# Two graph-attention layers: bias and beta added two batches ahead, key sums added by pairs, and VectorE's pieces moved within the step

## The chip, the cores and the metric

The kernel runs on one core of one Trainium2 chip. The core has a matrix engine (TensorE, PE in the profile), a vector engine (VectorE, DVE), a scalar engine (ScalarE, ACT), a general engine (GpSimd, POOL) and SyncE (SP), which here issues DMAs and waits. Each works through its own queue in order. The metric is the device time of one execution in microseconds (us).

## What is computed

`x` has 8 batches of 2048 nodes with 256 features, and one 2048 x 2048 adjacency matrix (`adj`, 0 or 1) serves all of them. Two layers follow each other, all in float32. Cut to what matters:

```python
# layer 0: attention with 4 heads of 64, softmax within each chunk of 256 keys, summed over the 8 chunks
h = maximum(layernorm(x), 0)
q, k, v = h @ Wq.T + bq, h @ Wk.T + bk, h @ Wv.T + bv
scores = clip(q.k / 8, -10, 10);  scores = where(adj == 0, -10, scores)
attn = softmax(scores, within the chunk);  ctx = sum over chunks of attn @ v
out = ctx @ Wo.T + bo + h
x = x + layernorm(out) * gamma + beta
# layer 1: one head, softmax over all keys
h = maximum(layernorm(x), 0) @ W
e = leaky_relu(h.a1 [of the node] + h.a2 [of the key]);  e = where(adj == 0, -1e9, e)
x = x + relu(softmax(e) @ h)
```

## The kernel before, in words

Batches run one after another, each in three stretches. **Attention** (layer 0) has 32 steps `n`: four blocks of 512 queries (`nb`) times eight chunks of 256 keys (`j`). **The passage** finishes the last block and makes layer 1's features while the next batch's queries, keys and values are computed. **Layer 1's products** take 16 pieces, four blocks of 512 queries times four groups of 512 keys.

The order on every engine is written out by hand in the body of the function. A step of attention does, for each of the four heads: the logits (PE, L502) into a two-bank PSUM tile `ps_s`, of which there are two; the clip against the bounds, which carry the mask (DVE, `clip`, L549), into a tile `e` of 2 x 512 per partition (11 in a ring, `ES`); the exponential in place (ACT, L557); and the addition of the two key halves (POOL, `add`, L564) into `g`. One DMA that accumulates, issued by POOL (`fold`, L569), adds one half of the partitions to the other; PE sums over partitions (L539); ACT makes reciprocals (`invert`, L575, L576). PE multiplies by the values (L517), DVE scales (`scale`, L588), and for all chunks but a block's first another accumulating DMA of POOL (`gather`, L592) adds the product `prod` to `ctxT`.

These are staggered: `begin(f)` and `end(f)` are the halves of step f. In them stand clips 3 of step f-1 and 0 of step f (begin), clips 1 and 2 of step f (end), and sums and values of step f-2. Each half calls a list of *pieces*, work of other stretches put beside attention. A piece with place 2f+2 stands in `begin(f)`, one with 2f+3 in `end(f)`; a plain piece stands at the end of its half, behind the half's two clips, and in `end` also behind the scaling. The places of a block's pieces are counted from 16 places after the block's first (`Between.beside`, `at((nb + 1) * PER + n)`).

The pieces of a finished block (class `Between`) are: load of x (-3), `residual`, a second normalization of x (ACT, L375; 3 and 4), `bias` (POOL, L756; 5 and 6), `beta` (POOL, L778; 8 and 10), the output projection (PE, L735; 9 and 10), `take`, which adds the projection to the biased features (DVE, L749; 10), statistics (DVE, L351 and L352; 11 and 12), `gamma` (DVE, L767; 14 and 15), scaling (ACT, L774), `add` to x (POOL, L782; 18 and 20), then layer 1's statistics, normalization and `flip1`, a transpose of 32 x 32 squares (DVE, L138; 30 and 31), and `send1`, which puts them into DRAM. The last block's pieces stand around the end of attention. In batch 0, further pieces prepare batch 1 (`beats`: load, statistics, normalization, flip, send) and turn the rest of the adjacency.

SP issues the loads, among them the bounds of the next block (L176, 1 MB, `fetch`), and carries in each step two empty instructions (`fence`, L471) that wait for PE's accumulator groups, so that SP keeps pace with PE.

In layer 1's products, DVE makes weights two pieces ahead: `weights` (L966: max of two scaled rows; L970: mask) into two tiles `e` of 2 x 512 per piece. PE multiplies (L988), and after each block `finish` divides, applies relu (ACT, L1009) and adds to x (POOL, L1011). Beside them the batch two ahead (`far`) is loaded into a tile `xp`, normalized, flipped and sent to DRAM; x is loaded again when its block is finished. The last four pieces also carry the first step of the next batch's attention (`early`).

Of the kernel before, what the change touches and what calls it, by code (L numbers as in the profile page):

```python
# [26 lines left out]
ES = 11  # L27
# [3 lines left out]
def gnn_two_layers(  # L31
# [96 lines left out]

    class Turning:
# [48 lines left out]

    def store_bounds(nb):
        nc.sync.dma_start(bound_d[nb], bounds[nb])  # L180
# [21 lines left out]
    def load_x(b, nb, tag, bufs):  # L202
        if tag == "g":
            if nb == 0:
                of_setup.append(g_tile())
            t = of_setup[0][:, nb * TB * F:(nb + 1) * TB * F].rearrange("p (t f) -> p t f", t=TB)
        else:
            t = xpool.tile([P, TB, F], F32, tag=tag, name=tag, bufs=bufs)
        nc.sync.dma_start(t, x[b, nb * NB:(nb + 1) * NB, :].rearrange("(p t) f -> p t f", p=P))
        return t  # L210
# [3 lines left out]
    def hn_tile(name="hn"):  # L214
        return work.tile([P, 2, F], F32, tag="hn", name=name, bufs=5)
# [59 lines left out]
    def missing_of(rows, t, half):  # L275

        tag = "e" if in_setup[0] else "hn"
        z = work.tile([P, 2 if in_setup[0] else 1, HALF], BF16, tag=tag, name="z", bufs=ES if tag == "e" else 5)
# [109 lines left out]
    class Projection:  # L388
        def __init__(self, b):
            self.b = b  # L390
            self.q = self.k = self.v = None
            self.adder = nc.vector
            self.x, self.mv, self.rn, self.hns, self.hT, self.pt = ({} for _ in range(6))

        def load(self, nb):
            self.x[nb] = load_x(self.b, nb, *(("g", 1) if in_setup[0] else ("xp", 1)))
# [6 lines left out]
        def power(self, nb):  # L403
            norm_power(self.mv[nb], self.rn[nb])

# [72 lines left out]
    class Attention:  # L478
# [28 lines left out]
        def values(self, n, half, turn, kt):  # L507
# [7 lines left out]
            for h in range(HEADS):  # L515
                at = h * DH + c * Q
                made.append(nc.tensor.matmul(  # L517
                    self.num[n, c][h * Q:(h + 1) * Q, :], self.v[rows, j * KT + kt, at:at + Q],
                    self.e[n, self.ORDER.index((h // 2, h % 2))][rows, kt, :],
                    start=turn == 0 and kt == 0, stop=turn == 1 and kt == KT - 1,  # L520
                ))
# [22 lines left out]
        def clip(self, n, o):  # L544
            if not self.has(n):
                return
            nb, j = self.STEPS[n]
            self.e[n, o] = work.tile([P, KT, NB], F32, tag="e", name="e", bufs=ES)
            nc.vector.scalar_tensor_tensor(  # L549
                self.e[n, o], self.s.pop((n, o)), -CLIP * SC,  # L550
# [3 lines left out]
        def exponentials(self, n, o):  # L554

            if self.has(n):
                nc.scalar.activation(self.e[n, o], self.e[n, o], AF.Exp, scale=1.0 / SC)  # L557

        def add(self, n, o):

            if self.has(n):
                p, i = self.ORDER[o]
                e = self.e[n, o]
                nc.gpsimd.tensor_tensor(self.both(n)[:, 2 * p + i, :], e[:, 0, :], e[:, 1, :], op=ALU.add)  # L564
# [25 lines left out]
        def gather(self, n):  # L590
            if self.has(n) and self.STEPS[n][1] > 0:
# [40 lines left out]
        def begin(self, f, pieces=()):  # L632
# [15 lines left out]
            if f == 1:  # L648
                for o in range(3):
                    self.add(0, o)  # L650
            self.add(f - 1, 3)
            self.fold(f - 1)
            if odd:
                self.slots(f, "o10", "v11", "o11", "o20")
            else:
                self.slots(f, "o10", "s00", "o11", "o20")
                self.add(f, 0)
            self.run(pieces, None)

        def end(self, f, pieces=()):  # L660
            odd = f % 2
            self.run(pieces, "first")
            if odd:
                self.slots(f, "s00", "o21", "v20", "v30", "v21", "v31")
                self.add(f, 0)
# [7 lines left out]
            self.add(f, 1)  # L673
# [8 lines left out]
            self.gather(f - 2)  # L682
            self.add(f, 2)
# [10 lines left out]
    class Between:  # L694
# [6 lines left out]
        def load(self):  # L701
            self.x4 = load_x(self.proj.b, self.nb, "x", NNB)

        def residual(self, t2):
            self.hn0[t2] = normed(self.x4, self.proj.rn[self.nb], t2)
# [39 lines left out]
        def take(self, t2):  # L745
            if t2 == 0:
                self.o4 = work.tile([P, TB, F], F32, tag="o4", name="o4", bufs=1)
                self.mv, self.rn = norm_tiles("rn", 2 * NNB)
            nc.vector.tensor_tensor(  # L749
                self.o4[:, 2 * t2:2 * t2 + 2, :], self.pp[t2].rearrange("p (i f) -> p i f", i=2),  # L750
                self.hn0[t2], op=ALU.add,
            )

        def bias(self, t2):
            hn = self.hn0[t2]
            self.adder.tensor_tensor(hn, hn, bo_r[:, None, :].to_broadcast([P, 2, F]), op=ALU.add)  # L756
# [19 lines left out]
        def beta(self, t2):  # L776
            x2 = self.x4[:, 2 * t2:2 * t2 + 2, :]
            self.adder.tensor_tensor(x2, x2, beta_r[:, None, :].to_broadcast([P, 2, F]), op=ALU.add)  # L778
# [77 lines left out]
        def beside(self):  # L856
# [8 lines left out]
                9: [pe1(lambda: self.output_tiled(0))],  # L865
                10: [
                    pe(lambda: self.output_tiled(1)), lambda: self.take(0), lambda: self.take(1),
                    lambda: self.beta(1),
                ],
                11: [lambda: self.stats([0, 1])],  # L870
                12: [lambda: self.stats([2, 3])],
                13: [self.power],
                14: [lambda: self.gamma([0, 1])],
                15: [lambda: self.gamma([2, 3])],
                16: [lambda: self.scaled(range(TB))],
                18: [lambda: self.add(0)],
                20: [lambda: self.add(1)],
# [5 lines left out]
            if self.nb == NNB - 2:  # L883
                return todo
            at(22, lambda: self.stats1([0, 1]))
            at(24, lambda: self.stats1([2, 3]))
            at(26, self.power1)
            at(27, self.shift1)
            at(28, lambda: self.norm1(0))
# [13 lines left out]
    class Layer1:  # L903
# [39 lines left out]
        def source(self, nb, of_keys):  # L943
            self.src[nb] = work.tile([P, NB], F32, tag="hn", name="src", bufs=5)
# [15 lines left out]
        def weights(self, nb, j4):  # L960
            made = []
            for i in range(2):
                w = work.tile([P, 2, NB], F32, tag="e", name="w", bufs=ES)
                at = 4 * j4 + 2 * i
                for j in (at, at + 1):
                    nc.vector.tensor_scalar(  # L966
                        w[:, j - at, :], self.src[nb], self.cd[:, 0, j:j + 1], self.cd[:, 1, j:j + 1],
                        op0=ALU.mult, op1=ALU.max,
                    )
                nc.vector.scalar_tensor_tensor(  # L970
                    w, bounds1[nb][:, at:at + 2, :], 0.0, w, op0=ALU.is_gt, op1=ALU.mult
                )
                made.append(w)
            return made
# [6 lines left out]
        def products(self, accs, w, j4):  # L981
# [4 lines left out]
            for i, t in pairs:  # L986
                j = 4 * j4 + i
                nc.tensor.matmul(  # L988
                    accs[t][:, 0:F + 1], w[i // 2][:, i % 2, t * P:(t + 1) * P], g[0][:, j, :],
# [153 lines left out]
    for b in range(B):  # L1143
# [25 lines left out]
        if b == 0:  # L1169
# [3 lines left out]
            beats = [(12, 13, 18, 19), (31, 32, 33, 34), (44, 46, 47, 48), (57, 58, 59, 60)]  # L1173
            for nb, ns in enumerate(beats):
                at(ns[0] - 5, lambda nb=nb: ahead.load(nb))
                for t, n in enumerate(ns):
                    at(n, lambda nb=nb, t=t: ahead.stats(nb, [t]))
                n = ns[-1]
                at(n + 1, lambda nb=nb: ahead.power(nb))
                at(n + 2, lambda nb=nb: ahead.shift(nb))  # L1180
                at(n + 3, lambda nb=nb: ahead.norm(nb, 0))
                at(n + 4, lambda nb=nb: ahead.norm(nb, 1))
                at(n + 4, lambda nb=nb: ahead.flip(nb, 0))
                at(n + 5, lambda nb=nb: ahead.flip(nb, 1))
                at(n + 7, lambda nb=nb: ahead.send(nb))
        else:
            at(6, lambda: fetch(bounds, 1))
        at(PER + 4, lambda: fetch(bounds, 2))
        at(2 * PER + 4, lambda: fetch(bounds, 3))
        at(3 * PER + 4, lambda: fetch(bounds1, 0))  # L1190
        at(STEPS2 + 2, lambda: fetch(bounds1, 1))
        at(STEPS2 - 6, last.load)
        at(STEPS2, lambda: last.residual(0))

        late = 0 if ahead else 2
        at(STEPS2 + 1 + late, lambda: last.residual(1))
        at(STEPS2 + 2, lambda: last.bias(0))
        at(STEPS2 + 3 + late, lambda: last.bias(1))
        at(STEPS2 + 4, lambda: last.beta(0))
        at(STEPS2 + 5, lambda: last.beta(1))  # L1200
# [147 lines left out]
        for i, (nb, j4) in enumerate(pieces1):  # L1348
# [21 lines left out]
            if far and i in (3, 6, 9, 12):  # L1370
                far.send(i // 3 - 1)
            if far and i in (0, 3, 6, 9):
                far.load(i // 3)
            if far and i in (1, 4, 7, 10):
# [48 lines left out]
```

## Time and profile before

| what | value |
|---|---|
| median of 3 runs | 3776.11 us (3771.88 to 3776.38) |
| the profiled execution | 3785.24 us, span 3783.5 us |
| granted TensorE clock | 0.984 |
| busy: PE, DVE, POOL, ACT | 3549.0, 2715.3, 2066.2, 1948.6 us |
| attention of batch 2, first to last clip | 295.1 us (1018.9 to 1314.0) |
| passage of batch 2 | 70.5 us (1314.0 to 1384.5) |
| layer 1's products of batch 2, to the next batch's first clip | 93.9 us (1384.5 to 1478.4) |

In the profile's group lines, after the operation and its tiles (out<-in), come the shapes (partitions x elements), the count, the union of the busy times in us, the mean of one in ns, and the idle time of the engine just before the group with what ended most of it. In a timeline come start, length, engine, line, operation, tiles and count; the bracket has the idle time before and who ended it. In a list of waits come the waiting instruction, whom it waited for, the sum in us, how often, and the longest. In a table of stretches the busy times of PE, PEld (weight loads), DVE, ACT and POOL follow the length, and last come the granted clock, the busy share of the DMA engines and GB/s.

### The profile page before, as it was taken

To read this page: it belongs to the slowest core of one execution; us is meant where nothing else is said; L and a number is where in the kernel's file an instruction comes from. 1 tells how busy PE (TensorE), PEld (TensorE's weight loads), DVE (VectorE), ACT (ScalarE), POOL (GpSimd) and SP (SyncE) were. 2 spreads that over 40 slices of the span, in tenths; PEclk is the share of its full clock that TensorE was granted. 3 is DMA by queue.
4 is the path that set the end of the run, shared out by engine and by line. 5 is a ranking of instruction groups with operands and counts; after the bars stand their busy time and mean duration, and the time that the engine had idled before them with its cause. 6 is when DMAs were issued, how large, how long until landed. Compare 5 with 4: busy or idle time off the path is not lost. (4 is left out here: it accounts for less than half of the span.)

```text
span 3783.5 us, 101129 instructions
## 1 busy us (share of the span) xinstructions
PE 3549.0 (94%) x44032; PEld 2085.4 (55%) x44032; DVE 2715.3 (72%) x4083; ACT 1948.6 (52%) x2929; POOL 2066.2 (55%) x1885
## 2 busy tenths in 40 slices
PE   8998999989999999998999999999999999999989
PEld 4334684446844477444764448644485445854458
DVE  6878586785768766786767767677676775757856
ACT  5666425674266632676336753366623665146641
POOL 3777107881088811887038860388504884058831
PEclk9999999999999999999999999999999999999989
DMA  7777526674367742777427764377643766147731
GB/s 225 160 147 152 112 92 127 127 148 99 92 135 140 156 92 76 153 140 155 99 72 146 147 141 89 88 136 146 141 97 89 148 130 143 56 85 146 145 78 51
DMA packets 189580, 463.76 MB, mean 123 GB/s; under 512 B 39760, under 2 KB 101456, under 8 KB 164560
## 3 DMA queue, kind: packets, MB, share of 16 engines
q0 software_dynamic: 53120, 252.74, 37.5%
q1 hardware_dynamic: 127696, 203.51, 18.9%
q8 instruction: 345, 5.65, 0.6%
q10 hardware_dynamic: 8320, 1.05, 0.2%
q14 instruction: 99, 0.81, 0.1%
HBM read 154.14 MB, written 51.43 MB: 54 GB/s over the span
## 5 line engine op out<-in xcount | busy, mean ns | idle before, releaser
L564 POOL TENSOR_TENSOR g<-e 128x512 f32<-128x512 f32 x1024 | 1466.5, 1483 | 473.2 <-ACT e L557 218.1
L502 PE MATMUL ps_s<-q,k 64*32 64x512 f32 x16384 | 1511.2, 602 | 90.6 <-DVE e L549 89.9
L549 DVE SCALAR_TENSOR_TENSOR e<-ps_s,bound 128x1024 f32<-128x1024 f32 x1024 | 1215.0, 1218 | 517.0 <-PE ps_s L502 497.4
L557 ACT ACTIVATE e<-e 128x1024 f32<-128x1024 f32 x1024 | 1064.7, 1053 | 666.4 <-DVE e L549 638.9
L517 PE MATMUL ps_n<-e,v 64*32 64x512 f32 x16384 | 1374.9, 601 | 12.3 <-ACT r L1009 7.6
L502 PEld LDWEIGHTS ps_s<-q,k 64*32 64x32 f32 x16384 | 469.1, 107 | 669.0 <-issue 300.0
L517 PEld LDWEIGHTS ps_n<-e,v 64*32 64x32 f32 x16384 | 472.7, 108 | 433.6 <-issue 246.8
L988 PE MATMUL ps_s<-g,w 128*128 128x257 f32 x2048 | 448.0, 380 | 0.0
L588 DVE TENSOR_TENSOR prod<-ps_n,rz 128x512 f32<-128x512 f32 x448 | 287.6, 684 | 192.7 <-PE ps_n L517 89.4
L988 PEld LDWEIGHTS ps_s<-g,w 128*128 128x128 f32 x2048 | 389.1, 190 | 56.2
L539 PE MATMUL ps_t<-g,ones 64*32 64x512 f32 x2048 | 284.1, 622 | 95.7 <-DMA g<-g 91.3
L363 POOL TENSOR_TENSOR krn<-krn,mv 128x4 f32<-128x4 f32 x28 | 6.6, 237 | 589.4 <-DVE w L966 589.4
L970 DVE SCALAR_TENSOR_TENSOR w<-bound,w 128x1024 f32<-128x1024 int8 x256 | 314.7, 1229 | 8.7
L1011 POOL TENSOR_TENSOR x<-x,r 128x256 f32<-128x256 f32 x124 | 92.0, 786 | 408.1 <-ACT r L1009 407.3
L988 PE MATMUL ps_n<-g,w 128*128 128x257 f32 x1024 | 292.4, 382 | 0.0
L988 PE MATMUL ps_t<-g,w 128*128 128x257 f32 x1024 | 289.7, 379 | 0.0
L966 DVE TENSOR_SCALAR w<-src,cd 128x512 f32<-128x512 f32 x512 | 263.3, 556 | 7.0 <-ACT src L945 6.6
L575 ACT ACTIVATE rz<-ps_t 128x512 f32<-128x512 f32 x256 | 151.0, 590 | 220.0 <-PE ps_s L502 124.8
L569 POOL DMA_DIRECT2D g<-g x256 | 212.8, 831 | 78.9 <-POOL g L564 63.8
L592 POOL DMA_DIRECT2D ctxT<-prod x224 | 206.0, 920 | 76.7 <-DVE prod L588 57.1
L988 PEld LDWEIGHTS ps_n<-g,w 128*128 128x128 f32 x1024 | 192.9, 190 | 44.3 <-issue 17.6
L988 PEld LDWEIGHTS ps_t<-g,w 128*128 128x128 f32 x1024 | 193.8, 189 | 28.2
(133 smaller groups left out, 3004.7 us busy)
## 6 DMA issues: line engine op xcount, KB each, us to landing
g<-g POOLq DMA_DIRECT2D x256, 512.0 KB, 5.6
ctxT<-prod POOLq DMA_DIRECT2D x224, 512.0 KB, 5.2
bound<-bound_d SPq DMA_DIRECT2D x62, 1024.0 KB, 6.9
turned_d<-squares SPq DMA_DIRECT2D x232, 128.0 KB, 2.4
hT<-turned_d SPq DMA_DIRECT2D x58, 512.0 KB, 4.0
rows<-in_adj_dram SPq DMA_DIRECT2D x32, 512.0 KB, 5.6
x<-in_x_dram SPq DMA_DIRECT2D x32, 512.0 KB, 4.5
out_dram<-x SPq DMA_DIRECT2D x31, 512.0 KB, 2.6
```

Of the source, the lines that this page charges most:

```text
L502: nc.tensor.matmul(self.s[n, o][c * Q:(c + 1) * Q, kt, :], self.k[p][rows, at:at + Q], self.q[p][rows, nb * NB:(nb + 1) * NB], start=True, ...
L517: made.append(nc.tensor.matmul(self.num[n, c][h * Q:(h + 1) * Q, :], self.v[rows, j * KT + kt, at:at + Q], self.e[n, self.ORDER.index((h / ...
L539: nc.tensor.matmul(self.total[n][h * Q:(h + 1) * Q, :], ones[rows, :], self.both(n)[rows, h, :], start=True, stop=True,)
L549: nc.vector.scalar_tensor_tensor(self.e[n, o], self.s.pop((n, o)), -CLIP * SC, bounds[nb][:, j * KT:(j + 1) * KT, :], op0=ALU.max, op1=ALU ...
L557: nc.scalar.activation(self.e[n, o], self.e[n, o], AF.Exp, scale=1.0 / SC)
L564: nc.gpsimd.tensor_tensor(self.both(n)[:, 2 * p + i, :], e[:, 0, :], e[:, 1, :], op=ALU.add)
L569: nc.gpsimd.dma_start(self.both(n)[mine], self.both(n)[other], accum_op=ALU.add)
L588: nc.vector.tensor_tensor(dst[:, c, :], self.num.pop((n, c)), self.rz[n], op=ALU.mult)
L592: nc.gpsimd.dma_start(self.ctxT[self.STEPS[n][0]], self.prod.pop(n), accum_op=ALU.add)
L966: nc.vector.tensor_scalar(w[:, j - at, :], self.src[nb], self.cd[:, 0, j:j + 1], self.cd[:, 1, j:j + 1], op0=ALU.mult, op1=ALU.max,)
L970: nc.vector.scalar_tensor_tensor(w, bounds1[nb][:, at:at + 2, :], 0.0, w, op0=ALU.is_gt, op1=ALU.mult)
L988: nc.tensor.matmul(accs[t][:, 0:F + 1], w[i // 2][:, i % 2, t * P:(t + 1) * P], g[0][:, j, :], start=j == 0, stop=j == NT - 1,)
```

## The change

It has four parts, and what follows from them.

- **Bias and beta.** While layer 1's products of batch b run, the normalized features and the x of batch b+2 get `bo` and `beta` added on POOL (`ready`) and are stored in DRAM (`keep_ready`, tensors `hb` and `xb`). A finished block of batches 1 to 7 then loads `hb` into `o4` (`features`, place 7) and `xb` into `x4` (`load`), and `residual`, `bias` and `beta` fall away there. `take` adds the projection to `o4` in place. For batch 1, x is loaded and normalized once more in layer 1 of batch 0. In batch 0 normalization and both additions stay, at other places.
- **Pairs.** A tile `e` holds both heads of a pair (4 x 512; 6 in the ring). In odd steps POOL adds the key halves of each pair in one instruction of 128x1024; in even steps it does so for pair 0 and keeps two single ones for pair 1. The gather of even steps moves from `end(f)` to behind the fold of `begin(f + 1)`.
- **Pieces of VectorE.** Statistics, `gamma` and the flips now stand in `begin` halves (places 12 and 14, 16 and 18, 30 and 32). In batch 0 the statistics for batch 1 are made by ACT (`moments`).
- **Bounds in parts.** The fetches within attention go out in four parts of 256 KB, one in every second half step.

A tile `xp` is no longer kept: x of the batch ahead goes into the rings `e` (layer 1) or `hT` (batch 0's attention). The weights of a piece are one tile of 4 x 512. The diff, cut to its core:

```diff
-ES = 11
+ES = 6
+    def fetch_part(of, nb, part):
+        if part == 0:
+            of[nb] = bound_tile()
+        four = slice(part * NT // 4, (part + 1) * NT // 4)
+        nc.sync.dma_start(of[nb][:, four, :], bound_d[nb][:, four, :])
...
+        def moments(self, nb, part):
...
+                for t in tiles:
+                    nc.scalar.activation(self.scratch[:, t % 2, :], x[:, t, :], AF.Copy, accum_out=mv[:, t, 0:1])
...
+        def ready(self, nb):
+            x = self.x[nb]
+            for t2 in range(2):
+                two = slice(2 * t2, 2 * t2 + 2)
+                hn, x2 = self.hns[nb][t2], x[:, two, :]
+                nc.gpsimd.tensor_tensor(hn, hn, bo_r[:, None, :].to_broadcast([P, 2, F]), op=ALU.add)
+                nc.gpsimd.tensor_tensor(x2, x2, beta_r[:, None, :].to_broadcast([P, 2, F]), op=ALU.add)
+        def keep_ready(self, nb):
+            d = ready_d[self.b % 2]
+            for t2 in range(2):
+                nc.sync.dma_start(d["hb"][nb][:, 2 * t2:2 * t2 + 2, :], self.hns[nb][t2])
+            nc.sync.dma_start(d["xb"][nb], self.x[nb])
...
-        def add(self, n, o):
+        def add(self, n, p, i=None):
             if self.has(n):
-                nc.gpsimd.tensor_tensor(self.both(n)[:, 2 * p + i, :], e[:, 0, :], e[:, 1, :], op=ALU.add)
+                e = self.e[n, p].rearrange("p (i k) q -> p k i q", k=KT)
+                heads = slice(0, 2) if i is None else slice(i, i + 1)
+                nc.gpsimd.tensor_tensor(
+                    self.both(n)[:, 2 * p:2 * p + 2, :][:, heads, :], e[:, 0, heads], e[:, 1, heads], op=ALU.add
+                )
...
         def begin(self, f, pieces=()):
-            self.add(f - 1, 3)
-            self.fold(f - 1)
+            if odd:
+                self.add(f - 1, 1, 0)
+                self.fold(f - 1)
+                self.gather(f - 3)
+            else:
+                self.add(f - 1, 1)
+                self.fold(f - 1)
...
         def end(self, f, pieces=()):
-            self.add(f, 1)
+            self.add(f, 0)
...
-            self.gather(f - 2)
-            self.add(f, 2)
+            if odd or not self.has(f + 1):
+                self.gather(f - 2)
+            else:
+                self.add(f, 1, 1)
...
-                3: [lambda: self.residual(0)],
-                4: [lambda: self.residual(1)],
-                5: [lambda: self.bias(0)],
-                6: [lambda: self.bias(1)],
-                8: [lambda: self.beta(0)],
-                11: [lambda: self.stats([0, 1])],
-                12: [lambda: self.stats([2, 3])],
-                14: [lambda: self.gamma([0, 1])],
-                15: [lambda: self.gamma([2, 3])],
+                7: [self.features],
+                12: [lambda: self.stats([0, 1])],
+                14: [lambda: self.stats([2, 3])],
+                16: [lambda: self.gamma([0, 1])],
+                17: [lambda: self.scaled([0, 1])],
+                18: [lambda: self.gamma([2, 3]), lambda: self.add(0)],
+                19: [lambda: self.scaled([2, 3])],
...
-            at(31, lambda: self.flip1(1))
+            at(32, lambda: self.flip1(1))
...
-        at(PER + 4, lambda: fetch(bounds, 2))
+        for part in range(4):
+            at(PER + 4 + 2 * part, lambda part=part: fetch_part(bounds, 2, part))
...
             if far and i in (3, 6, 9, 12):
                 far.send(i // 3 - 1)
+                far.ready(i // 3 - 1)
+            if far and i in (4, 7, 10, 13):
+                far.keep_ready(i // 3 - 1)
...
+            if b == 0 and i in (3, 6, 9, 12):
+                for t2 in range(2):
+                    ahead.norm(i // 3 - 1, t2)
+                ahead.ready(i // 3 - 1)
```

More of the change, by code (lines that the diff above doesn't have):

```diff
@@ L127, in gnn_two_layers @@
     }
+    ready_d = [
+        {name: [kept.tile([P, TB, F], F32, name=f"{name}_d{i}_{nb}") for nb in range(NNB)] for name in ("hb", "xb")}
+        for i in range(2)
+    ]
     class Turning:
@@ L943, in source @@
         def source(self, nb, of_keys):
-            self.src[nb] = work.tile([P, NB], F32, tag="hn", name="src", bufs=5)
+            self.src[nb] = work.tile([P, NB], F32, tag="hn", name="src", bufs=HS)
             nc.scalar.activation(
@@ L960, in weights @@
         def weights(self, nb, j4):
[L961 to L968, printed above, removed]
-                    )
[L970 to L974, printed above, removed]
+            w = work.tile([P, 4, NB], F32, tag="e", name="w", bufs=ES)
+            for i in range(4):
+                j = 4 * j4 + i
+                nc.vector.tensor_scalar(
+                    w[:, i, :], self.src[nb], self.cd[:, 0, j:j + 1], self.cd[:, 1, j:j + 1],
+                    op0=ALU.mult, op1=ALU.max,
+                )
+                if i % 2:
+                    two = w[:, i - 1:i + 1, :]
+                    nc.vector.scalar_tensor_tensor(
+                        two, bounds1[nb][:, j - 1:j + 1, :], 0.0, two, op0=ALU.is_gt, op1=ALU.mult
+                    )
+            return w
         def accumulators(self, nb):
@@ L1191, in gnn_two_layers @@
+        for part in range(4):
+            at(PER + 4 + 2 * part, lambda part=part: fetch_part(bounds, 2, part))
+            at(2 * PER + 4 + 2 * part, lambda part=part: fetch_part(bounds, 3, part))
+            at(3 * PER + 4 + 2 * part, lambda part=part: fetch_part(bounds1, 0, part))
         at(STEPS2 + 2, lambda: fetch(bounds1, 1))
         at(STEPS2 - 6, last.load)
-        at(STEPS2, lambda: last.residual(0))
-        late = 0 if ahead else 2
-        at(STEPS2 + 1 + late, lambda: last.residual(1))
@@ L1197, in gnn_two_layers @@
[L1197 to L1200, printed above, removed]
+        at(STEPS2 + 5, last.features)
+        for t2 in range(2):
+            at(STEPS2 + 3 + t2, lambda t2=t2: last.beta(t2))
+            at(STEPS2 + 5, lambda t2=t2: last.bias(t2))
         at(STEPS2 + 3, low.fetch1)
```

148 lines of the change are left out of this document (92 added, 56 removed).

## The prediction, made before the changed kernel ran

> **What bounds the kernel now.** I read the page first, then who waited for whom on PE, then one batch in stretches, then single waits in order of time.
>
> ```profile
> PE 3549.0 (94%) x44032; PEld 2085.4 (55%) x44032; DVE 2715.3 (72%) x4083; ACT 1948.6 (52%) x2929; POOL 2066.2 (55%) x1885
> ...
> L564 POOL TENSOR_TENSOR g<-e 128x512 f32<-128x512 f32 x1024 | 1466.5, 1483 | 473.2 <-ACT e L557 218.1
> ...
> L539 PE MATMUL ps_t<-g,ones 64*32 64x512 f32 x2048 | 284.1, 622 | 95.7 <-DMA g<-g 91.3
> ```
>
> TensorE bounds the kernel. What can be won without less TensorE work is its idle time, 234 us, and PE's own waits say who causes it: the fold that adds two halves of the softmax sums (L569, awaited by L539), and VectorE's clips, which must free a PSUM bank before the next logits (L502).
>
> ```profile
> PE ps_t L539 <- DMA g<-g: 91.3, 69, 6.4
> PE ps_s L502 <- DVE e L549: 89.9, 68, 3.4
> ```
>
> By stretches, batch 2: attention (first to last clip), the passage, and layer 1's products.
>
> ```profile
> 1018.90:1314.00 295.10, 273.36 (x4660) 136.75 (x4660) 218.54 (x262) 186.38 (x239) 233.02 (x205) 0.99 0.66 130
> 1314.00:1384.50 70.50, 66.75 (x349) 41.32 (x350) 29.85 (x77) 35.37 (x81) 13.45 (x13) 1.00 0.56 118
> 1384.50:1478.40 93.90, 93.90 (x458) 80.67 (x456) 84.24 (x164) 17.66 (x42) 9.38 (x16) 1.00 0.37 101
> ```
>
> After each length come the busy times of PE, PEld, DVE, ACT, POOL. Attention has 21.7 us of PE idle and a POOL at 79%. In layer 1 PE has none, POOL is nearly free, but DVE is at 90%: the change moves POOL work there.
>
> An idle microsecond costs more than itself. Eight of the small matmuls start every 0.43 us; at that pace attention's need about 255 of the 295.1 us, so 40 are lost where 21.7 are idle. [...] I count a wait taken away at 1.3 to 1.4 times its length (between 1 and 40/21.7 = 1.8).
>
> Where the two waits come from:
>
> ```profile
> 1101.95 0.32 SPq L176 DMA_DIRECT2D bound<-bound_d  x1
> ...
> 1103.73 0.83 POOL L569 DMA_DIRECT2D g<-g  x1 [0.30 <-POOL g L564]
> ...
> 1112.13 0.63 PE L539 MATMUL ps_t<-g,ones 64*32 64x512 f32 x4 [1.59 <-DMA g<-g]
> ```
>
> This fold was issued 1.78 us behind a 1 MB fetch of bounds and landed after 8.27 us; with no fetch in its way one takes 5.11. The batch has three such waits (1.59, 1.51, 1.03 = 4.1 us). Three more (0.88, 0.34, 0.69 = 1.9) follow steps in which additions of bias, beta and x stand on POOL ahead of the key sums: there the fold goes out some 3 us after the last exponential, where 1.69 is usual. The rest, an x load and the stretch's start, stays.
>
> ```profile
> 1159.19 2.85 DVE L767 SCALAR_TENSOR_TENSOR o<-o,mv,gamma_r 128x256 f32<-128x256 f32 x2
> 1161.96 2.34 DVE L549 SCALAR_TENSOR_TENSOR e<-ps_s,bound 128x1024 f32<-128x1024 f32 x2
> ```
>
> ```profile
> 1163.23 0.63 PE L502 MATMUL ps_s<-q,k 64*32 64x512 f32 x4 [2.32 <-DVE e L549]
> ```
>
> Two gamma pieces stand between the second and the last clip of a step, and PE waits 2.32 us. Alone one takes 0.47 us; beside a POOL addition it is held until that ends (0.91 in the mean of all). The batch has three such waits (2.32, 2.71, 2.99) and three of 0.62 behind statistics: 9.9 us.
>
> **The change, part by part.** Sums are against the profiled execution, 3785.24 us (span 3783.5 and 1.7 around it), 9.1 above the median of 3776.11.
>
> *Bounds in four parts* (31 fetches of attention; the batch's three above among them). They are spaced, since SP carries a fence (L471) for every accumulator group and waited 1900 us in all at them. A quarter takes about a quarter of the fetch's 3.2 us from a fold: 4.1 falls to about 1.2 per batch.
>
> *Bias and beta out of attention.* 64 additions at L756 (1575 ns) and 64 at L778 (1543) were on POOL, four per block; batch 0's 16 stay. So 1.9 falls to about 0.2. ACT loses four normalizations per block (587 ns each), which were hidden. In their place each of 28 blocks fetches o4, 0.5 MB more on SP's queue beside a fold. An x load of that size made the fold at 1079.54 land after 7.25 us and cost 1.45; others cost nothing. I take 0.3 each, **8 us** (0 to 40).
>
> Fold together: (2.9 + 1.7) x 1.3 = 6 per batch, seven batches, **-42** (0 to -70).
>
> *Pairs.* 1024 additions become 384 of 128x1024 and 256 of 128x512; the trace has no such pair. A lone 128x512 takes 1.31, a lone 128x256 0.73, so the slope gives 2.5; two queued ones take 2.82. POOL gains 0.3 per pair, but is not the last in a steady step. For odd steps the fold then follows the last exponential by 2.8 rather than 1.7, which the half step until their sums covers: such folds landed 3 to 5 us early with no fetch in the way. Even steps, which have no such room, keep a single last addition, and their gather moves behind the fold. Zero, with 0.3 per step (77 us for 256) as the bad end and the POOL time won back as the good one, inside the fold's -70.
>
> *VectorE's pieces behind the first clips.* Statistics, gamma and flips now follow the two clips that begin a step, and the next bank is wanted later. There L767's pair took 1.94 us at 1153.87 with no wait of PE after it. New is that in even steps the second gamma pair stands beside a pair addition, and can be held 2.5 instead of 1.3: I leave 2 us per batch of 9.9. 7.9 x 1.4 = 11 per batch, **-76**; batch 0, whose statistics for batch 1 go from DVE (32 operations) to ACT, had 20.0 us of this wait in attention and I take half, **-10** (together 0 to -125).
>
> *Larger e tiles, fewer.* Six of 4x512 for eleven of 2x512, and none for xp. A clip needs the tile of three steps ago, released before its logits: zero. In layer 1 three weights and two x tiles share the six; covered by VectorE's lead, below.
>
> *Additions in layer 1.* 28 blocks x 4 additions of 128x512: 24 blocks beside the products of batches 0 to 5 for the batch two ahead, and 4 more, for batch 1, in batch 0's. POOL is free, but VectorE's weights are held meanwhile:
>
> ```profile
> 1469.45 3.11 POOL L1011 TENSOR_TENSOR x<-x,r 128x256 f32<-128x256 f32 x4 [9.76 <-ACT r L1009]
> ```
>
> ```profile
> 1470.99 1.85 DVE L966 TENSOR_SCALAR w<-src,cd 128x512 f32<-128x512 f32 x2
> ...
> 1474.02 1.00 DVE L966 TENSOR_SCALAR w<-src,cd 128x512 f32<-128x512 f32 x2
> ```
>
> Two L966 lost 0.86 us to about 1.54 of POOL time, 56%. One block's additions are 4 x 1.31 = 5.2 us, so DVE loses 2.9 (0 if they fall on statistics and transposes, 5.2 if all is lost). Weights lead the products by 7 to 15 us, which covers it. The first thing late is the passage to the next batch: the clips of its step 0 stand behind weights(15), and PE takes them after the next products.
>
> ```profile
> 1478.48 2.35 DVE L549 SCALAR_TENSOR_TENSOR e<-ps_s,bound 128x1024 f32<-128x1024 f32 x2 [2.20 <-PE ps_s L502]
> ```
>
> They end at 1480.83 and are wanted at 1485.50: with the 2.20 idle before, 6.9 us to spare. Four blocks make 11.6, a stall of 4.7 in batches 1 to 5; batch 0, with eight, 23.2 - 6.9 = 16. **+40** (0 to 5 x 13.9 + 35 = 104).
>
> The rule here is in the Trainium skill, "Advanced Engine Details and Errata", section VectorE Performance Modes: the second VectorE port is shared with GpSimd, and the instructions of one block those of the other. It names no share. Read as all of the time lost it gives the 104; the row's 56% gives the 40, and I go by the row.
>
> Stores of the prepared tiles (28 MB) fall on layer 1, whose DMA engines are 37% busy: zero.
>
> Sum: -42 - 76 - 10 + 8 + 40 = -80: 3705.2 profiled, and 9.1 less by the median: **3696 us**.
>
> **Rivals.**
> 1. *The held weights stay covered* (additions fall on statistics and transposes): -128 + 8 = -120, 3656. For it: 7 to 15 us of lead. Against: DVE is at 90% there. Chance 0.25.
> 2. *The forecast*, 3696, its own range 3672 to 3728. 0.42.
> 3. *Attention gives half*: the even folds, which have almost no room, become the limit as soon as VectorE is not. -64 + 48 = -16 to, with the additions covered, -56: 3720 to 3760, say 3745. For it: even folds often land 0.14 us before their sums start. 0.18.
> 4. *Slower: POOL's hold on VectorE costs its full price.* All of an addition's time is lost to the weights (+104), and a gamma piece behind a 2.5 us pair addition waits so long that PE's clip waits come back (the -86 gone): -42 + 8 + 104 = +70, 3846. With the clip waits back it turns slower from 2.7 us of hold per block (28 holds less the 41.4 to spare reach 34); with them gone only from 5.8. Against: the 56%, and that the DMA issue behind an odd step's single addition leaves the port free. 0.12.
> 5. *The parts go out together*, SP being ahead: 2.9 x 1.3 x 7 = 26 less won, 3722. Against: the fences. 0.03.
>
> **How the numbers follow.** 0.2% (7.6 us) is about what a measurement of this kernel can tell from no change. Rivals 1, 2, 5 and most of 3 are faster: 0.83; a slim part of 3 falls within: 0.04; 4 and what I have not seen: 0.13. The range takes in 1 with some room below, all of 2, 3 and 5, and leaves out 4: 3638 to 3785.
>
> **What would show it.** PE's wait for the fold falls from 91.3 to about 55, that for the clips from 89.9 to about 50, less what the end of layer 1 adds; POOL's key sums show 384 pairs near 2.5 us; the folds behind bounds land in 6 us instead of 8; the weights' L966 and L970 grow in the mean, and a wait of PE for the first clips of each batch appears while layer 1's last products run, longest in batch 0. I am wrong if the sums' wait stays near 91, if that first-clip wait passes 15 us in every batch, or if a steady pair of steps becomes longer than now.

## The result, and the profile after

The changed kernel takes 4029.32 us (median of 4 runs, 4027.72 to 4040.25), the kernel before 3776.24 (4 runs): a ratio of 1.068 (95% interval 1.066 to 1.070), 253 us slower. The forecast was 3696, 80 us faster, and its range ended at 3785. The profiled execution took 4029.38 us, its span 4027.6.

The page of the changed kernel; the columns are those explained with the profile before:

```profile
PE 3626.2 (90%) x44032; PEld 2082.3 (52%) x44032; DVE 2880.3 (72%) x4051; ACT 1920.9 (48%) x2897; POOL 2034.2 (51%) x1501
...
L622 POOL TENSOR_TENSOR g<-e 128x1024 f32<-128x1024 f32 (+1 forms) x640 | 1290.6, 2084 | 474.3 <-ACT e L615 309.5
...
L593 PE MATMUL ps_t<-g,ones 64*32 64x512 f32 x2048 | 300.2, 655 | 293.7 <-DMA g<-g 249.2
...
L652 POOL DMA_DIRECT2D ctxT<-prod x224 | 220.2, 983 | 405.3 <-DMA ctxT<-prod 93.6
...
ctxT<-prod POOLq DMA_DIRECT2D x224, 512.0 KB, 6.3
```

TensorE is idle for 401 us where it was for 234. POOL has less to add, as was meant (its key sums, L622, fell from 1466.5 to 1290.6 us), and nothing is won by it: POOL now stands idle for 405 us in front of the gathers. Before, the gather's two rows read:

```profile
L592 POOL DMA_DIRECT2D ctxT<-prod x224 | 206.0, 920 | 76.7 <-DVE prod L588 57.1
...
ctxT<-prod POOLq DMA_DIRECT2D x224, 512.0 KB, 5.2
```

PE's waits in the changed kernel (waiting instruction, whom it waited for, sum in us, times, longest):

```profile
PE ps_t L593 <- DMA g<-g: 249.2, 99, 7.1
PE ps_t L593 <- POOL g L622: 38.7, 13, 5.0
PE ps_s L556 <- DVE e L605: 32.6, 26, 2.6
PE ps_s L556 <- ACT r L1080: 26.2, 7, 6.6
```

The third row is what the change was to bring: the clips' wait fell from 89.9 to 32.6. The first is what it cost: the sums' wait rose from 91.3 to 249.2. The last row did not exist before; it belongs to layer 1.

**Where the time goes, step by step.** A stretch of batch 2 in the changed kernel, in order of time:

```profile
1222.11 0.81 POOL L629 DMA_DIRECT2D g<-g  x1 [0.30 <-POOL g L622]
1222.66 1.17 POOL L652 DMA_DIRECT2D ctxT<-prod  x1
...
1225.05 2.44 POOL L622 TENSOR_TENSOR g<-e 128x1024 f32<-128x1024 f32 x1 [1.22 <-ACT e L615]
...
1227.37 2.19 ACT L615 ACTIVATE e<-e 128x1024 f32<-128x1024 f32 x2 [1.46 <-DVE e L605]
...
1231.04 0.86 POOL L652 DMA_DIRECT2D ctxT<-prod  x1 [3.55 <-PE ps_s L556]
...
1231.63 2.69 POOL L622 TENSOR_TENSOR g<-e 128x1024 f32<-128x1024 f32 x1
...
1234.62 0.83 POOL L629 DMA_DIRECT2D g<-g  x1 [0.30 <-PE ps_s L556]
...
1239.87 0.94 PE L593 MATMUL ps_t<-g,ones 64*32 64x512 f32 x4 [2.90 <-DMA g<-g]
```

The gather of an even step goes out at 1222.66, right behind a fold, and lands at 1230.49, 7.8 us later. The next gather adds into the same `ctxT` and must not start before. Its product is ready at 1225.74, yet it is issued at 1231.04, 0.55 us after that landing. (The bracket names PE's logits, with which a gather has nothing to do; where the named engine can't be the reason, it was another, here the DMA.) POOL works in order, so the pair's addition and the fold behind it wait too, although the last exponential they need ended at 1228.42 (the first of the two in the row of ACT): the fold lands at 1239.73, and PE, 2.90 us idle, takes the sums at 1239.87. By the trace's DMA records, 88 of the 192 gathers that follow another into the same tile start 0.3 to 0.8 us after its landing, against 6 before. The gathers of steps 2, 4 and 6 of a block land 8.3, 8.0 and 7.8 us after their issue (5.0, 4.9, 6.7 before); the folds land as they did (5.76 us in even and 5.79 in odd steps, from 5.74 and 6.27).

**What an idle microsecond costs.** These stretches of the same step show it (length, then busy times of PE, PEld, DVE, ACT, POOL, granted clock, DMA share, GB/s):

```profile
1236.90:1239.87 2.97, 0.07 (x5) 0.03 (x2) 2.97 (x1) 0.00 (x0) 2.97 (x3) 1.00 0.71 132
1239.87:1243.30 3.43, 3.43 (x40) 1.40 (x48) 3.36 (x4) 1.54 (x3) 2.12 (x3) 0.53 0.54 79
```

PE stands idle for 2.90 of these 2.97 us, and for the next 3.43 it is granted about half its clock (0.53). Over the whole trace, a stretch at half clock began within 5 us of the end of 53 of 56 idle stretches of PE of 3 us or more, of 9 of 29 between 2 and 3 us, and of 2 of 64 between 0.5 and 2 us. The Trainium skill, "TensorE: Matmul & The Clock Gate", section Why this matters for your kernels, advises against gaps of more than about 3 us between matmuls for this reason; the trace agrees. In the kernel before it was 5 of 6, 17 of 32 and 10 of 98, so 3 us is no sharp limit here. So every span in this text is split in three: PE's idle time (span less PE's busy time), the clock's loss (span times the missing share of the clock), and the rest.

| kernel | span | idle | clock | rest |
|---|---|---|---|---|
| before | 3783.5 | 234.5 | 61 (0.984) | 3488 |
| changed | 4027.6 | 401.4 | 153 (0.962) | 3473 |

Of 244 us more, 167 are idle time and 92 the clock. Half clock that falls into idle time is counted in both columns; counted only while PE is busy, the clock's loss is 56 and 134 us, 78 more, and the rest is the same in both kernels (3493 and 3492).

### The profile page after: what moved, and what is told of

It is laid out like the page before. It is cut to its first block, busy times and chain, and to the rows that moved or that the text cites. A ratio compares the mean times of both kernels' runs of the same rounds, so it can differ in the third digit from the quotient of the medians.

```text
span 4027.6 us, 101085 instructions
## 1 busy us (share of the span) xinstructions
PE 3626.2 (90%) x44032; PEld 2082.3 (52%) x44032; DVE 2880.3 (72%) x4051; ACT 1920.9 (48%) x2897; POOL 2034.2 (51%) x1501
## 5 line engine op out<-in xcount | busy, mean ns | idle before, releaser
L556 PE MATMUL ps_s<-q,k 64*32 64x512 f32 x16384 | 1539.1, 606 | 60.5 <-DVE e L605 32.6
L622 POOL TENSOR_TENSOR g<-e 128x1024 f32<-128x1024 f32 (+1 forms) x640 | 1290.6, 2084 | 474.3 <-ACT e L615 309.5
L571 PE MATMUL ps_n<-e,v 64*32 64x512 f32 x16384 | 1390.9, 627 | 8.8 <-ACT r L1080 7.6
L556 PEld LDWEIGHTS ps_s<-q,k 64*32 64x32 f32 x16384 | 463.6, 108 | 637.1 <-issue 340.3
L593 PE MATMUL ps_t<-g,ones 64*32 64x512 f32 x2048 | 300.2, 655 | 293.7 <-DMA g<-g 249.2
L652 POOL DMA_DIRECT2D ctxT<-prod x224 | 220.2, 983 | 405.3 <-DMA ctxT<-prod 93.6
L1042 DVE SCALAR_TENSOR_TENSOR w<-bound,w 128x1024 f32<-128x1024 int8 x256 | 345.8, 1351 | 8.8
L1036 DVE TENSOR_SCALAR w<-src,cd 128x512 f32<-128x512 f32 x512 | 325.3, 677 | 7.0 <-ACT src L1017 6.6
L593 PEld LDWEIGHTS ps_t<-g,ones 64*32 64x32 f32 x2048 | 56.6, 108 | 431.8 <-POOL g L622 277.2
```

What stands on the lines that cost most here:

```text
L556: nc.tensor.matmul(self.s[n, o][c * Q:(c + 1) * Q, kt, :], self.k[p][rows, at:at + Q], self.q[p][rows, nb * NB:(nb + 1) * NB], start=True, ...
L571: made.append(nc.tensor.matmul(self.num[n, c][h * Q:(h + 1) * Q, :], self.v[rows, j * KT + kt, at:at + Q], self.e[n, h // 2][rows, h % 2 * ...
L593: nc.tensor.matmul(self.total[n][h * Q:(h + 1) * Q, :], ones[rows, :], self.both(n)[rows, h, :], start=True, stop=True,)
L622: nc.gpsimd.tensor_tensor(self.both(n)[:, 2 * p:2 * p + 2, :][:, heads, :], e[:, 0, heads], e[:, 1, heads], op=ALU.add)
L652: nc.gpsimd.dma_start(self.ctxT[self.STEPS[n][0]], self.prod.pop(n), accum_op=ALU.add)
L1036: nc.vector.tensor_scalar(w[:, i, :], self.src[nb], self.cd[:, 0, j:j + 1], self.cd[:, 1, j:j + 1], op0=ALU.mult, op1=ALU.max,)
```

## The experiments

**1. The gather back in its place** (the changed kernel otherwise):

```diff
         def begin(self, f, pieces=()):
             if odd:
                 self.add(f - 1, 1, 0)
                 self.fold(f - 1)
-                self.gather(f - 3)
...
         def end(self, f, pieces=()):
-            if odd or not self.has(f + 1):
-                self.gather(f - 2)
-            else:
+            self.gather(f - 2)
+            if not odd and self.has(f + 1):
                 self.add(f, 1, 1)
```

> The changed kernel, but the gather of even steps stands again in end(f), in front of the single key-sum addition. Theory A (the moved gather lands late behind the fold, the next gather into the same ctxT must wait for its landing, and POOL, standing in that wait, sends the odd fold late): the odd gathers' 395 us of idle before them go, PE's wait for the fold falls from 249 us to 60 or less, and the time to 3640 to 3730. Theory B (pairs make the odd folds late): still above 3950. Theory C (the additions in layer 1 hold VectorE): still above 3900.

Measured: 3808.93 us, 1.0075 of before (1.0048 to 1.0102). 220 of the 253 us are gone, the clock is 0.981, and 11 gathers instead of 88 start right behind a landing. So theory A names the main cause, but the time is in no theory's range, and the sums' wait stays at 117.9 us where 60 or less were expected. The kernel is still not faster than before; the rest of the forecast had failed too, by less.

**2. Only the gather moved, in the kernel before** (the same edit in the other direction).

> The kernel before, with one edit: the gather of even steps moves behind the fold of the next begin. Theory A: this edit alone costs what the change cost, 3930 to 4050, with odd gathers starting 0.55 us after the landing of the one before. Theories B and C: within 20 us of the kernel before.

Measured: 4025.9 us, 1.0654 (1.0621 to 1.0687). This one move, with nothing else changed, makes the kernel as slow as the whole change did: 245 us here, 220 in the changed kernel, whose other parts cost 28 in sum (experiment 1). POOL's idle time before gathers is 460.9 us, and PE waits:

```profile
L592 POOL DMA_DIRECT2D ctxT<-prod x224 | 223.8, 999 | 460.9 <-PE ps_n L517 164.2
```

```profile
PE ps_t L539 <- DMA g<-g: 258.7, 118, 8.5
PE ps_s L502 <- DVE e L549: 68.8, 63, 4.2
```

**3. The gather in the same half step, ahead of the addition and the fold.**

```diff
             if odd:
+                self.gather(f - 3)
                 self.add(f - 1, 1, 0)
                 self.fold(f - 1)
-                self.gather(f - 3)
```

> The changed kernel with the gather of even steps in the same half step, but ahead of that half's single addition and fold instead of behind them. Theory A (what costs is that the next gather, which accumulates into the same ctxT, must wait for this one's landing, and this one lands late because it stands behind the fold): issued about 2 us earlier and with no fold ahead of it, it lands near 5 us after issue instead of 8, POOL's idle time before gathers falls from 405 us to below 150, and the time to 3800 to 3880 (3809 is the kernel with the gather fully back; the odd folds still go out 0.9 us later behind it). Rival (any place in the next step costs as much, since the two gathers still stand three quarters of a step or less apart): 3950 or more.

Measured: 3868.5 us, 1.0235 (1.0199 to 1.0271), inside the first theory's 3800 to 3880. POOL's idle time before gathers fell to 124 us, and gathers land after 5.5 us in the median; those of steps 2, 4 and 6, the moved ones, after 6.7, 5.2 and 6.5 in the mean (8.3, 8.0 and 7.8 behind the fold):

```profile
L652 POOL DMA_DIRECT2D ctxT<-prod x224 | 187.2, 836 | 123.8 <-DVE prod L648 43.2
...
ctxT<-prod POOLq DMA_DIRECT2D x224, 512.0 KB, 5.5
```

So it is the landing that the next gather waits for, made late by the fold in front. A quarter of the gathers (47) still start right behind a landing, and the fold now stands behind the gather: the sums' wait is 158.2 us, 117.9 with the gather fully back.

**4. Every head added by itself** (on experiment 1: the pair's one instruction of 128x1024 becomes two of 128x512 at the same place).

```diff
-                heads = slice(0, 2) if i is None else slice(i, i + 1)
-                nc.gpsimd.tensor_tensor(self.both(n)[...][:, heads, :], e[:, 0, heads], e[:, 1, heads], op=ALU.add)
+                for one in (1, 0) if i is None else (i,):
+                    nc.gpsimd.tensor_tensor(self.both(n)[:, 2 * p + one, :], e[:, 0, one], e[:, 1, one], op=ALU.add)
```

> As the kernel with the gather put back, and each pair addition of 128x1024 is two of 128x512. It tells what pairs are worth. Theory A: within 25 us of the pairs' time, either way (0.3 us of POOL per pair, not last in a step). Theory B: well below the pairs' time, by 100 us or more.

Measured: 3742.79 us, 0.9907 (0.9877 to 0.9937): 66 us less than with pairs, between the two theories (25 at most, 100 or more). The waits of PE with pairs, and then without:

```profile
PE ps_t L593 <- DMA g<-g: 117.9, 79, 6.3
PE ps_s L556 <- DVE e L605: 35.1, 38, 2.5
```

```profile
PE ps_t L593 <- DMA g<-g: 94.8, 69, 5.6
...
PE ps_s L556 <- DVE e L605: 22.8, 20, 1.9
```

Two prices appear. A pair can't start before both its exponentials are done, so in odd steps the fold follows the last exponential by 2.91 us instead of 1.95 (means of 128), in even steps by 3.13 instead of 2.87; the sums' wait grows by 0.10 us per step in both. And an addition of twice the length holds VectorE longer: the 128 gamma pieces take 130 us instead of 116, and the clips' wait grows by 12.

**5. Pairs in odd steps alone** (on experiment 1).

```diff
+                for heads in ([slice(1, 2), slice(0, 1)] if i is None and n % 2 == 0 else [heads]):
                     nc.gpsimd.tensor_tensor(
```

> The changed kernel with the gather back in its place, the pair addition in odd steps alone; even steps add every head by itself. With all pairs it was 3809, with none 3743: 66 us to share out. Theory A: the cost is in odd steps, whose fold goes out 2.9 us after the last exponential instead of 1.95: the time stays at 3790 to 3815. Theory B: it is in even steps, whose fold has no room and comes later since the pair cannot start until both exponentials are done: 3740 to 3765, with PE's wait at the sums near 95 instead of 118. Theory C, both alike: about 3775.

Measured: 3783.66 us, 1.0008 (0.9989 to 1.0026): between the theories. 41 of the 66 us belong to odd steps, 25 to even ones. The clips' wait is already 34.0, so that share belongs to odd steps' pairs; the sums' wait is 100.4.

**6. No additions in layer 1** (on experiment 1; bias and beta are then missing from batches 1 to 7).

```diff
         def ready(self, nb):
-                nc.gpsimd.tensor_tensor(hn, hn, bo_r[...], op=ALU.add)
-                nc.gpsimd.tensor_tensor(x2, x2, beta_r[...], op=ALU.add)
```

> As the kernel with the gather put back, but the additions of bias and beta in layer 1 are left out (bias and beta are missing from batches 1 to 7). It measures the term that I put at 40 us. Theory A: 25 to 60 us below the kernel with the gather put back; the first-clip waits behind layer 1 (26 us in the changed kernel) vanish and the weights' two instructions return to 556 and 1229 ns. Theory C: more than 150 below.

Measured: 3740.3 us, 0.9901 (0.9862 to 0.9940), 69 us less than with them; 40 had been forecast, 25 to 60 expected. The weights are back at 557 and 1229 ns, and the wait for ScalarE ahead of the next batch's logits, 27.0 us in experiment 1, is down to 0.2. What the additions do is best seen in the kernel of experiment 4, which has them too. At the end of layer 1's third block:

```profile
1454.70 0.81 PE L1057 MATMUL ps_s<-g,w 128*128 128x257 f32 x3
...
1463.60 1.23 DVE L1040 SCALAR_TENSOR_TENSOR w<-bound,w 128x1024 f32<-128x1024 int8 x1
1464.75 0.15 DVE L1075 TENSOR_SCALAR rz<-ps_s 128x1 f32<-128x1 f32 x1
...
1466.62 5.01 PE L556 MATMUL ps_s<-q,k 64*32 64x512 f32 x32 [4.16 <-ACT r L1078]
```

```profile
1462.46:1466.62 4.16, 0.00 (x1) 0.01 (x1) 3.12 (x10) 1.00 (x3) 0.72 (x1) 0.87 0.29 73
1466.62:1475.90 9.28, 9.28 (x42) 4.46 (x43) 8.79 (x8) 0.83 (x2) 8.71 (x7) 0.50 0.30 115
```

The third block's last product ends at 1455.5. VectorE starts its division (L1075) only at 1464.75, since it has fallen behind by its weights of three blocks. Then ScalarE's relu (L1078) empties `ps_s`, into which the next batch's first logits (L556) are to go 7 us after that product: PE waits 4.16 us, and then runs for 9.28 us at half clock. In the kernel before, the first of these logits start 6.9 us behind the third block's products without a wait.

**7. Only the bias added in layer 1** (beta is missing from batches 1 to 7):

```diff
-                nc.gpsimd.tensor_tensor(x2, x2, beta_r[...], op=ALU.add)
```

> The changed kernel with the gather back in its place and only bo added in layer 1 (beta is left out of batches 1 to 7). With both additions 3809, with none 3740. Theory A, a threshold: VectorE falls behind by 3.3 us per block; what it delays first is the division of the third block, which frees the logits' PSUM banks and has 7 us to spare; three half holds make 5 us, so PE's waits of 4 us before each batch's first logits go, and the half clock behind them: 3740 to 3756. Theory B, in proportion: half of 69, 3770 to 3780.

Measured: 3754.22 us, 0.9944 (0.9926 to 0.9962): a threshold, not a proportion. Half the additions cost a fifth to a quarter of all of them (16 us by the ratios, 14 by the medians, of 66 and 69), and the wait is left in batch 0 alone, which prepares two batches:

```profile
PE ps_s L555 <- ACT r L1077: 5.3, 1, 5.3
```

**8. VectorE's pieces alone** (the kernel before with the places of statistics, gamma and flips taken from the change's diff, nothing else).

> The kernel before with one part of the change alone: VectorE's statistics, gammas and flips at their new places (bias, beta, pairs, bounds and the gather stay as before). Theory A (the prediction's term, without batch 0's share of 10): PE's wait for the clips falls from 90 us to about 25 and the time by 60 to 95 us, to 3685 to 3720. Theory B (the folds of even steps, which have no room, become the limit as soon as VectorE is not): the clip wait falls as much, PE's wait at the sums rises from 91 to 120 or more, and the time falls by 40 us or less, to 3735 or above.

Measured: 3710.13 us, 0.9815 (0.9790 to 0.9839): 70 us won, 76 had been forecast. The clips' wait is 20.9 us; the sums' wait rose to 102.6, less than theory B's 120.

**9. Bounds in parts alone** (the kernel before with `fetch_part` in place of `fetch` within attention).

> The kernel before with the bounds of attention fetched in four parts and nothing else. Theory A (the prediction: 2.9 us of fold waits less per batch, seven batches, times 1.3): the wait at the sums falls from 91 to about 70 and the time by 20 to 30 us, to 3746 to 3756. Theory B (four small fetches slow more folds by a little than one large one slowed by much): the wait at the sums stays within 8 of 91 and the time within 8 us of before.

Measured: 3760.23 us, 0.9942 (0.9920 to 0.9964): 20 us won, 26 had been forecast. The sums' wait is 67.0 us.

**10. Both** (8 and 9 in one kernel, nothing else of the change).

> The kernel before with both of these parts and nothing else of the change. If they add up as the prediction had them: 3660 to 3700, the fastest so far. If the folds of even steps are the limit that both run into: within 15 us of the better of the two alone. Against the changed kernel with the gather back and single additions (3743) it lacks the additions in layer 1, for which the run without them measured about 69 us: by that it should be near 3675.

Measured: 3672.42 us (3669.77 to 3688.45), 0.9721 (0.9697 to 0.9745), 108 us faster than before and the fastest of all. The two at least add up: 70 and 20 would make 90, and whether the other 18 are real the three intervals leave open.

```profile
PE 3513.9 (96%) x44032; PEld 2038.0 (56%) x44032; DVE 2709.0 (74%) x4083; ACT 1958.4 (53%) x2929; POOL 2067.7 (56%) x1885
```

```profile
PE ps_t L545 <- DMA g<-g: 83.7, 74, 6.2
PE ps_s L508 <- DVE e L555: 20.3, 18, 2.1
```

**11. Batch 0's statistics for batch 1 on ScalarE, on top of that** (`moments` and its places from the change).

> The kernel before with VectorE's pieces and the bounds in parts (3672), and besides, as in the change, batch 0's statistics for batch 1 on ScalarE. The prediction's term: 10 us less, 3657 to 3667, with PE's wait for clips in batch 0 (17 of the 20 us of that wait are left there) about halved. Rival (these waits have another cause, the rest of the adjacency's transposes): within 4 us of 3672.

Measured: 3678.59 us, 0.9736 (0.9704 to 0.9768): nothing won that can be told from experiment 10. Batch 0's attention keeps its length (304.9 us, 304.8 without), and PE still loses 11.7 us there to clips, 11.2 without (the expectation's 17 was too high). What causes these waits was not tried.

**12. What is left of the change** with the gather back, single additions and none in layer 1 (bias and beta are missing from batches 1 to 7).

> What is left of the change when the gather is back, every head is added by itself and nothing is added in layer 1 (bias and beta are missing from batches 1 to 7): pieces, bounds in parts, batch 0 on ScalarE, and the prepared tiles loaded in place of the work on POOL in attention. The kernel before with pieces and parts alone took 3672. Theory A (the prediction: 17 won where no addition of bias, beta stands ahead of the key sums, 8 lost to the loads of o4): 3655 to 3667. Theory B (the loads and stores cost what the fewer additions win): 3668 to 3682, PE's wait at the sums near 85. If the costs found alone add up (66 for pairs, 69 for the additions, off 3809), it comes to 3674.

Measured: 3677.24 us, 0.9739 (0.9720 to 0.9758). Taking bias and beta out of attention, with all the loads and stores that this needs, moves nothing: 5 us beside experiment 10, inside the spread. The run also has the change's larger tiles `e`, another order of the key sums and batch 0 on ScalarE, so it shows their sum alone. The costs found one by one add up.

| from | to | us | idle | clock | rest |
|---|---|---|---|---|---|
| before | pieces and parts (10) | -108 | -80 | -28 | -8 |
| 10 | bias and beta out of attention, larger tiles, batch 0 on ScalarE (12) | +5 | +1 | 0 | +2 |
| 12 | additions in layer 1 (4) | +66 | +43 | +27 | 0 |
| 4 | pairs (1) | +66 | +33 | +12 | +17 |
| 1 | gather moved (the change) | +220 | +170 | +81 | -26 |

The first column of numbers is of medians (before: 3775.6 to 3781.0 in the four series), the others are of the profiled spans; the clock's counts half clock within idle time too, up to 8 us of a row. What makes the +17 and the -26 of the last two rows, which nearly cancel, the runs don't show.

## Why the prediction was wrong, point by point

- **The step that failed** is the term of the even steps' gather: "their gather moves behind the fold", priced at "Zero". It looked for the cost on POOL, whose work stays the same, and not at the transfer: two gathers of a block add into one tile, so each must land before the next may be issued. The trace of before had the numbers. In its time line of POOL, the fold that stands in the first half of an odd step, and the next gather, at the end of the same step:

```profile
1165.95 0.83 POOL L569 DMA_DIRECT2D g<-g  x1 [0.30 <-POOL g L564]
...
1171.41 0.84 POOL L592 DMA_DIRECT2D ctxT<-prod  x1
```

  Here they are 5.5 us apart, in the mean of all odd steps 4.6. The issue of the fold takes 0.6 of that, so a gather put behind it has 4 to 5 us until the next is due, and a gather lands after 5.2 in the median, later behind another transfer, as the folds behind bounds showed. The waits that follow, on POOL, then for the fold, then of PE, then the half clock, made +220 (experiments 1 to 3). No rival named it; the one on the slower side was VectorE's hold, which is real but of a third of that size.
- **Pairs, zero: +66.** "The half step until their sums covers" the later fold was read from folds that landed 3 to 5 us early; of the 128 odd steps' folds before, 35 landed 3 us or more ahead of their sums, and half less than 0.5 us. With the pieces moved, odd steps' folds land 1.39 us ahead of their sums in the mean (experiment 4), and more than half of the even steps' land just as they are wanted (0.14 us ahead). The bad end of that term, 77, was near the truth. Of the 62 us between the two spans, idle time and clock explain 45; what makes the other 17, in which PE counts as busy, the runs don't show.
- **Additions in layer 1, +40: +66 to +69.** The share of the hold was right: weights take 93 us longer per kernel (L966 556 to 677 ns, L970 1229 to 1351), 3.3 us per block, 2.9 had been taken. The idle time, 43 us, came out by luck: at the end of layer 1 batch 0 waits 6.6 us in the changed kernel, not 16, and batches 1 to 5 wait 3.9 each, not 4.7, which makes 26; the rest stands elsewhere. The place was wrong too: the first thing late is the division of the third block, with 7 us to spare, not the clips of the next step 0 with 6.9. And the half clock behind each wait, 27 us, wasn't priced (experiments 6 and 7).
- **VectorE's pieces, -76: -70. Bounds in parts, -26 of the -42: -20.** Right, each within 6 us, and together -108, so rival 3, that attention would give half, is out (experiments 8 to 10). The multiplier of 1.3 to 1.4, a choice between two bounds, came out too, for a reason that the prediction didn't give: 80 us of idle time less and 28 of clock are 1.35 times the idle time. The trace of before shows the half clock right behind the wait of 2.32 us that the prediction read (granted clock 0.50, third from the end):

```profile
1164.00:1167.40 3.40, 3.40 (x40) 1.34 (x36) 1.42 (x2) 2.92 (x6) 2.14 (x2) 0.50 0.15 22
```

  Two slips of the working cost little: 11 us a batch over seven batches is 77, not 76, and the wait given as 2.99 us is two, of 2.71 and 0.29.
- **Bias and beta out of attention, -16, and the loads of o4, +8; batch 0, -10.** None of them is to be seen: +5 in all (experiments 11 and 12). Batch 0's 20.0 us of clip waits fell to 11.8 with the moved pieces alone (experiment 8), and its statistics on ScalarE took nothing more. That other loads of x "cost nothing" was read from batch 2: over the whole trace of before, PE waited for 12 of the 24 folds issued just behind such a load, 0.15 to 1.67 us each. Whether small gains and costs cancel there was not tried apart.
- Two of the prediction's three signs of being wrong came: the sums' wait didn't fall, it rose to 249.2 us, and a steady pair of steps became longer (clip to clip 19.5 us in the mean, 17.6 before). The wait at the end of layer 1 stayed below its 15 us.

## What to carry to other kernels

When a DMA is moved, write down its landing as well as its issue, and ask which later instruction touches the same bytes: an accumulating transfer that must land before the next is issued blocks the issuing engine's whole queue, and everything behind it is late. Price a wait of TensorE of 2 to 3 us or more at its length and, where the granted clock shows it, half of the time at half clock that follows. And a change of several parts deserves a run of each: two of these parts win 108 us, the others lose 357.

## What the runs showed of the hardware

- A gather issued right behind a fold lands after about 8 us instead of 5 to 7, at the same size (0.5 MB), and the fold ahead of it isn't slowed (5.76 us, 5.74 before): the second transfer pays for both.
- The Trainium skill, "DMA: Bandwidth & Descriptors", section Two DMAs through the same engine are not ordered, says that a dependent DMA needs a wait of the issuing engine on the first one's completion. That is the wait seen here; its price in this kernel is 0.55 us from landing to issue, and 3.3 to 4.4 us of an idle queue in the mean of the gathers that had to wait (the block's steps 3, 5 and 7).
- An addition of 128x1024 on POOL takes 2.45 us in the median, two queued ones of 128x512 2.7 to 2.8 (medians of four kernels): a pair saves 0.2 to 0.4 us of POOL time and costs the earlier start of its first half.
